# New ranks for a kernel's queues: a two-layer transformer on one core, with warm-up transposes and first scores ahead of first values

## The chip, the core and the metric

The kernel runs on one core of a Trainium2 chip. A core has five instruction queues that run side by side and wait for each other through semaphores: TensorE (PE in the profile: matrix products and transposes through the array, with its weight loads as PEld), VectorE (DVE), ScalarE (ACT), GpSimd (POOL) and SyncE (SP, which here issues nearly all transfers; POOL issues the indirect ones). Each queue works strictly in the order in which the program lists its instructions.

The metric is the device time of one execution in microseconds (us). The kernel before took 1245.04 us, the median of 3 runs (1244.42 to 1253.15).

## What is computed

Two transformer layers over 4096 tokens (16 sequences of 256) of width 128, all in 32-bit floats. Both layers have attention and a mixture of 8 experts of which each token uses 2; a normalisation follows each of the four parts.

```python
x = L0_attn_x                                   # (16, 256, 128)
x = _layernorm(x + _L0_attn_ref(x, ...))        # 16 heads of 64, softmax over 256 keys
x = _layernorm(x + _L0_ffn_ref(x, ...))         # 8 experts 128 -> 256 -> 128, top 2, and a shared one
x = _layernorm(x + _L1_attn_ref(x, ...))        # over the 16 heads of 8 of one token
x = _layernorm(x + _L1_ffn_ref(x, ...))         # 8 experts 128 -> 512 -> 128, top 2
return x
```

Layer 0's attention begins with an RMS norm, scales q by 1/8 and is the usual one. Layer 1's is odd: the softmax of a token runs over its own 16 heads, so scores and sums are small products within one token and are done element by element on VectorE and GpSimd, not as matrix products on TensorE. The expert layers take, for each token, the two largest of eight router probabilities, and add the two experts' outputs with those weights.

## The kernel before

**Tiles.** The tokens lie in 8 groups of 512 (`xg[0]` to `xg[7]`), each as 128 partitions by 4 chunks. Layer 0's attention runs over units: 128 pairs (a pair of heads in one sequence), 16 to a group. A unit has scores on PE (`scores`, L557, into `s`), the row maximum on DVE (`nm`, L533), the exponential on ACT (`pr`, L539), a reciprocal on DVE (`rs`, L550), the scaling of `pr` by it on POOL (L554), eight transposes on PE (`turn`, L587), copies of these out of PSUM (`pT`), the product with the values (`attended`, `po`, L608) and its copy (`oT`). A unit's transposes and products are issued three units after its scores (`LAG = 3`). Copies out of PSUM go through `copied` (L258), which gives each one to DVE (L266) or ACT (L268), whichever the planner believes is free first.

**Experts.** Most tokens go through the expert layers in waves (`WAVES`): layer 0 has waves 0 to 3, layer 1 has waves 0 to 2. A wave is routed (`route`, some 30 small DVE steps that end in each token's row numbers `r_pi`, L848); `send` (L891) scatters each token's row twice into a list in DRAM by indirect DMAs from POOL (L900); `lists` (L964) works through that list in tiles of 128 rows, with each tile's expert weights fetched by SP at a register's address (`wa`, `wb`), transposes (`px`), first products (`ph`, L1093), the GELU on ACT, second products (`po_e`, L1113) and a store into `outs`; `gathered` (L915) brings each token's two results back by indirect DMAs from POOL (`y`, L929). Only one wave's list runs at a time. `shared` (L1148) is layer 0's shared expert. The last 256 tokens use all 8 experts densely instead (`sequence`, `dense`).

**Layer 1's attention.** `chunk1` (L1196) handles 128 tokens: products of q and k on DVE (`qk_prod`), their sums (`sc`), the maximum, its subtraction on POOL or DVE (L1240), the exponential, products with v on POOL or DVE (`av_prod`, L1287), their sums and the scaling. Where the heads are over (`"over" in end`) and PE is `SUMS` us behind DVE in the planner's clock, both kinds of sums may be matrix products with the identity instead.

**What sets the order.** The whole program is written out at build time by a planner. Every piece of work (a unit's softmax, a wave's routing, a copy) is a Python generator, a *strand*; at each `yield` it says when its next step could start and on which engine. `everything` (L318) takes again and again the strand with the smallest start, and issues its next step:

```python
best = min(starts, key=lambda c: (max(c[0] - c[1].key[0], first), c[1].key[1:]))[1]
```

Here `key[0]` is a head start in us and `key[1]` a rank that breaks ties, both from the table `KEYS` (L147) by the kind of work: `"softmax": (rank, time)`. `PACE` gives the rank of the heads' main strand for each half group, `COPY`, `FAVOUR`, `SWITCH` and `SWITCH_BACK` bias the choice between engines and the wish to change ACT's function table. The planner's clock advances by charges written in the code (`work("DVE", 2.3, at)`): they are not measured at run time, they only decide the order. What it issues to a queue stays in that order on the chip, whatever the real times are.

**The start.** SP loads `x0`, `wq`, `wk`, `wv` and the rest in a fixed order. `normalised` (L463) makes the first normalised tokens; PE transposes them (`t_h`, L489) and a copy makes `hT`; from it come q and k (`projected`, L502, `pq`, `pk`) and v (`values`, L520, `pv`). `prepared` (L437) scales `wq` on DVE and writes the routing's constants on POOL; both are already issued behind the first norm here. `attention0` (L662) is the heads' main strand.

Of the kernel before, what the change touches and what calls it, by code (L numbers as in the profile page):

```python
# [9 lines left out]
FP = mybir.dt.float32  # L10
# [5 lines left out]
P = 128  # L16
D = 128
NTOK = 16 * 256
GT = 512
# [18 lines left out]
def two_layers(  # L38
# [71 lines left out]
    ident = const.tile([P, P], FP, tag="ident", name="ident")  # L110
    make_identity(nc, ident)
    mhalf = const.tile([P, NC], FP, tag="mhalf", name="mhalf")
    nc.gpsimd.memset(mhalf, -0.5)
# [20 lines left out]
    def cleared(layer, w):  # L134
# [12 lines left out]
    KEYS = {  # L147
        "copy qk": (-0.47, 0.098),
        "copy v": (-1.837, 0.311),
        "copy p": (-0.447, 0.289),  # L150
        "copy o": (-1.827, 0.05),
        "softmax": (-0.929, 0.15),
        "softmax 2": (-1.083, 0.3),
        "summed": (-2, 0.423),
        "normalised": (0.064, 0.401),
        "heads": (-0.036, 0.211),
        "w route": (0.209, 0.074),
        "w send": (-1.218, 0.245),
        "w shared": (-0.01, 0.358),
        "w loads": (-0.331, 0.017),  # L160
        "w turns 0": (-1.333, 0.096),
        "w turns 1": (0.218, 0.164),
        "w firsts 0": (-1.281, 0.243),
        "w firsts 1": (-0.641, 0.323),
        "w gelu": (-0.628, -0.115),
        "w seconds 0": (-0.513, 0.357),
        "w seconds 1": (0.844, 0.265),
        "w stored": (0.739, 0.057),
        "w gathered 0": (0.711, 0.093),
        "w gathered 1": (-0.147, -0.105),  # L170
        "w qkv": (0.126, -0.312),
        "w attention1": (0.364, 0.299),
        "w attention1 2": (1.784, 0.157),
        "w sums": (0.147, 0.241),
        "w normed": (-1.691, 0.205),
        "d loads": (-0.333, 0.978),
        "d route": (0.685, 0.221),
        "d firsts": (-0.122, -0.8),
        "d gelu": (-1.017, 0.988),
        "d seconds": (-0.245, -0.179),  # L180
        "d added": (-0.775, 1.421),
        "d normed": (0.891, 0.233),
    }
    PACE = [-0.064, 2, 0.528, -1.037, -1.955, -0.986, 0.284, 1.781]
    PACE += [1.065, 0.72, 1.611, 1.611, 1.069, 1.069, 1.469, 1.415]
    now = [0]
    COPY = -0.0
    SUMS = 14.742
    FAVOUR = -0.033
    SWITCH, SWITCH_BACK = 0.42, 0.949  # L190
    window, unit = [0, 0.0, 1.0], [P]
# [188 lines left out]
    def normed(y, o, tag, at):  # L380
# [21 lines left out]
        nc.gpsimd.tensor_scalar(nb, nb, -1.0, 1.0, ALU.mult, ALU.mult)  # L402
        at = work("POOL", 0.5, at)
        for c in range(n):
# [32 lines left out]
    def prepared():  # L437

        yield 4.0, "DVE"
        nc.vector.tensor_scalar(wq_s, wq_s, DH**-0.5, None, ALU.mult)  # L440
        end["wq"] = work("DVE", 0.75)
        yield after(("h", 0)), "POOL"
        nc.gpsimd.iota(falling, pattern=[[-1, NE]], base=NE, channel_multiplier=0, allow_small_or_imprecise_dtypes=True)
        nc.gpsimd.memset(earlier, 1.0)
        nc.gpsimd.affine_select(
            earlier, earlier, pattern=[[1, P]], compare_op=ALU.is_gt, fill=0.0, base=0, channel_multiplier=-1
        )
        nc.gpsimd.memset(ones, 1.0)


        nc.gpsimd.tensor_tensor(earlier, earlier, ones, ALU.subtract)
        nc.gpsimd.memset(going, 1.0)
        nc.gpsimd.memset(going[:, :, 0:1], 0.0)
        nc.gpsimd.memset(both, 0.0)
        nc.gpsimd.memset(upto, 0.0)
        for e in range(NE):
            nc.gpsimd.memset(upto[:, e, 0 : e + 1], 1.0)
        nc.gpsimd.iota(count, pattern=[[1, NTM]], base=0, channel_multiplier=0, allow_small_or_imprecise_dtypes=True)
        nc.gpsimd.iota(count128, pattern=[[P, CM]], base=0, channel_multiplier=0, allow_small_or_imprecise_dtypes=True)
        nc.gpsimd.memset(clear, 0.0)  # L460
        end["prepared"] = work("POOL", 9.0)

# [199 lines left out]
    def attention0():  # L662
        yield from projected(0, 0, wq_s, "q", qT)
        yield from projected(0, 0, wk_s, "k", kT)
        for c in range(NC):
            yield from values(0, 0, c)
        clears = [(0, 0), (0, 1), (1, 0), (0, 2), (1, 1), (0, 3), (1, 2)]
        for u in range(len(UNITS) + LAG):
# [4 lines left out]
            if g < NG:  # L673
# [27 lines left out]
                if i == 1 and 0 < g < LAST:  # L701
                    yield from values(g, 0, 3)
                yield from scores(u)
            if u >= LAG:
                yield from attended(u - LAG)
# [41 lines left out]
    def chosen(r, lg, layer, C, at):  # L747
# [33 lines left out]
        for k in range(2):  # L781
# [7 lines left out]
            nc.vector.tensor_tensor(first[:, k], eq, best.unsqueeze(2).to_broadcast(full), ALU.is_equal)  # L789
            at = work("DVE", 1.0 + 0.03 * C, at)  # L790
            yield at, "DVE"
        return first, pb, at

    def route(r, lg, layer, C, NT, at):
# [53 lines left out]
        nc.vector.tensor_copy(r.pos, pos)  # L848
        r.at = at = work("DVE", 2.3, at)
        begin(send(r), key("w send", w))  # L850
# [13 lines left out]
        if layer == 0:  # L864
# [15 lines left out]
            nc.vector.tensor_tensor(r.w[:, :, 0:NE], m.rearrange("p e c -> p c e"), pb, ALU.mult)  # L880
            r.weighed = work("DVE", 1.8, at)

# [313 lines left out]
    def chunk1(w, c, o, qv, kv, at, sums):  # L1196
# [57 lines left out]
        def reciprocals(at):  # L1254
            yield at, "DVE"
            nc.vector.tensor_reduce(rs, sc1, AX.X, ALU.add)
            nc.vector.reciprocal(rs, rs)
            mine["rs"] = work("DVE", 0.6, at)

# [399 lines left out]
```

## Time and profile before

One execution was profiled. It took 1250.27 us; its span, from the first to the last instruction, is 1248.6 us, and the mean granted clock of PE is 0.943 of full speed.

| | PE | DVE | ACT | POOL |
|---|---|---|---|---|
| busy, us | 1104.1 | 878.0 | 736.9 | 680.5 |
| share of the span | 88% | 70% | 59% | 54% |
| share of the chain that ended last | 49% | 21% | 6% | 14% |

Some times of this execution: the first scores start at 16.4 us; the maximum of unit 48 is taken at about 251 us, just after wave 0 of layer 0 has been routed; that of the last unit, 127, at about 864; the last product of the heads' output ends at 881; layer 1's three waves are routed by 924, 1038 and about 1132 us.

The page's rows are read as follows. A digit in a row of 40 slices is the busy share of that slice in tenths (a slice is 31 us); the DMA row is the mean share of 16 transfer engines. A row of a group gives the source line, the engine, the operation, the tile written and the tiles read, shapes and count, then the total busy time, the mean of one in ns, and the idle time of the engine just before these instructions with what ended it. A busy PE is not PE at its peak, since products are pipelined. Idle time of an engine counts only where something waits for that engine.

### The profile page before, as it was taken

The numbers are of one execution on the slowest core, as the hardware profiler recorded it, in microseconds if no ns is written. First come the engines' busy times: TensorE is split into PE (matmuls) and PEld (weight loads), VectorE is DVE, ScalarE is ACT, GpSimd is POOL, SyncE is SP. The second block draws the span as 40 slices with busy tenths as digits, with TensorE's granted clock in tenths as the row PEclk, the third lists the DMA queues.
The fourth block names the chain that finished last, engine by engine and source line by source line (L and its number), as shares of the span: only waits on it lengthen the run. The fifth ranks groups of instructions, "written<-read, shape, count | busy, mean of one in ns | idle before, by whom it ended". The sixth has DMA issues, their size and how long they took to land.

```text
span 1248.6 us, 22246 instructions
## 1 busy us (share of the span) xinstructions
PE 1104.1 (88%) x7175; PEld 795.3 (64%) x7175; DVE 878.0 (70%) x1748; ACT 736.9 (59%) x2086; POOL 680.5 (54%) x1059
## 2 busy tenths in 40 slices
PE   7999999979999999888999778998577998887985
PEld 3566665647665566656665456765455887887885
DVE  3766677634268897298789988779888779784433
ACT  5656566546757866477666567665346556544443
POOL 4434344372186647333765653485758827557654
PEclk9999999989999999789999889998768999888998
DMA  9800000033310003133000304213526879677981
GB/s 267 246 1 1 2 2 1 1 119 102 102 35 6 1 1 96 40 94 98 28 8 1 100 28 137 73 31 103 174 83 190 271 217 287 198 212 215 263 250 57
DMA packets 181527, 129.23 MB, mean 104 GB/s; under 512 B 12442, under 2 KB 165795, under 8 KB 181411
## 3 DMA queue, kind: packets, MB, share of 16 engines
q1 hardware_dynamic: 173730, 112.06, 30.4%
q0 software_dynamic: 7680, 15.74, 4.0%
q8 instruction: 58, 0.95, 0.3%
q14 instruction: 59, 0.48, 0.1%
HBM read 95.64 MB, written 32.11 MB: 102 GB/s over the span
## 4 chain that ended last, share of the span: by engine, by line
PE 49%; DVE 21%; POOL 14%; ACT 6%; issue 5%; DMA 4%; SPq 0%; ACTq 0%; POOLq 0%; DVEq 0%
PE s L570 8%; PE po L608 7%; POOL rows L900 7%; PE t L587 7%; PE ph L1093 3%; PE pv L524 3%; PE po_e L1113 3%; DVE qk_prod L1211 3%; PE pq L506 3%; PE pk L506 3%; PE py L625 3%; DMA y<-outs,r_pi 3%; DVE o L1262 3%; DVE sc L1215 2%; ACT pr L539 2%
## 5 line engine op out<-in xcount | busy, mean ns | idle before, releaser
L554 POOL TENSOR_SCALAR pr<-pr,rs 128x256 f32<-128x256 f32 x512 | 254.9, 515 | 329.4 <-DVE rs L550 237.7
L539 ACT ACTIVATE pr<-s,nm 128x256 f32<-128x256 f32 x512 | 235.6, 476 | 18.3 <-DVE nm L533 15.7
L533 DVE TENSOR_REDUCE nm<-s 128x4 f32<-128x1024 f32 x128 | 155.6, 1218 | 71.4 <-PE s L570 70.6
L1093 PE MATMUL ph<-xqT,wa 128*128 128x128 f32 x1000 | 139.1, 296 | 22.7 <-ACT h L1072 7.0
L587 PE MATMUL t<-ident,pr 128*128 128x128 f32 x1024 | 144.3, 282 | 6.7 <-POOL pr L554 4.6
L929 POOL DMA_INDIRECT y<-outs,r_pi x120 | 122.2, 1018 | 51.3 <-issue 23.4
L900 POOL DMA_INDIRECT rows<-x,r_pi x120 | 131.9, 1099 | 33.2 <-issue 20.8
L1093 PEld LDWEIGHTS ph<-xqT,wa 128*128 128x128 f32 x1000 | 129.6, 206 | 30.8 <-ACT h L1072 11.5
L608 PE MATMUL po<-pT,v 128*64 128x256 f32 x1024 | 142.4, 394 | 7.7 <-DVE kT L266 2.4
L587 PEld LDWEIGHTS t<-ident,pr 128*128 128x128 f32 x1024 | 112.9, 143 | 52.3 <-POOL pr L554 29.6
L570 PEld LDWEIGHTS s<-kT,qT 64*128 64x128 f32 x896 | 77.1, 186 | 85.2 <-issue 72.9
L570 PE MATMUL s<-kT,qT 64*128 64x256 f32 x896 | 127.0, 402 | 0.8 <-ACT pr L539 0.8
L266 DVE COPY pT<-t 128x512 f32<-128x512 f32 x146 | 95.4, 684 | 43.0 <-PE t L587 42.7
L268 ACT COPY oT<-po 128x256 f32<-128x256 f32 x103 | 38.3, 372 | 128.2 <-PE po L608 128.2
L608 PEld LDWEIGHTS po<-pT,v 128*64 128x64 f32 x1024 | 64.0, 136 | 67.4 <-issue 18.7
L539 ACT ACTIVATION_READ_ACCUMULATOR pr<-s,nm 128x1 f32 x512 | 106.2, 207 | 0.0
L1287 POOL TENSOR_TENSOR av_prod<-sc,qkv 128x1024 f32<-128x1024 f32 x28 | 70.8, 2535 | 60.6 <-ACT sc L1249 49.7
L1211 DVE TENSOR_TENSOR qk_prod<-qkv 128x1024 f32<-128x1024 f32 x64 | 82.3, 1286 | 10.1 <-ACT qkv L268 9.9
L268 ACT COPY pT<-t 128x512 f32<-128x512 f32 x110 | 61.2, 589 | 38.3 <-PE t L587 38.1
L1262 DVE TENSOR_REDUCE o<-av_prod 128x64 f32<-128x1024 f32 x64 | 76.1, 1205 | 6.0 <-POOL av_prod L1287 5.7
L1215 DVE TENSOR_REDUCE sc<-qk_prod 128x128 f32<-128x1024 f32 x64 | 78.1, 1220 | 2.2
L1113 PE MATMUL po_e<-wb,h 128*128 128x128 f32 x648 | 77.9, 279 | 1.7 <-ACT h L1066 1.4
(229 smaller groups left out, 1966.9 us busy)
## 6 DMA issues: line engine op xcount, KB each, us to landing
wa<-in_w_dram SPq DMA_DIRECT2D x176, 128.0 KB
wa<-in_w_dram SPq DMA_DIRECT2D x81, 256.0 KB
wb<-in_w_dram SPq DMA_DIRECT2D x81, 256.0 KB
xq<-rows SPq DMA_DIRECT2D x37, 256.0 KB
outs<-yq SPq DMA_DIRECT2D x37, 256.0 KB
rows<-clear SPq DMA_DIRECT2D x4, 1472.0 KB
rows<-clear SPq DMA_DIRECT2D x1, 2496.0 KB
rows<-clear SPq DMA_DIRECT2D x2, 1216.0 KB
```

Source lines behind the costliest of these rows:

```text
L533: nc.vector.tensor_reduce(nm[u], s, AX.X, ALU.max, negate=True)
L539: nc.scalar.activation(pr[u][:, i, :], s[:, i, :], AF.Exp, bias=nm[u][:, i : i + 1], accum_out=su[u][:, i : i + 1],)
L554: nc.gpsimd.tensor_scalar(pr[u][:, i, :], pr[u][:, i, :], rs[:, i : i + 1], 1.0, ALU.mult, ALU.mult)
L570: nc.tensor.matmul(sc[u][:, j, qc, :], q[part, ts(qc, P)], k[part, :], start=True, stop=True,)
L587: nc.tensor.transpose(t[:, kc, ts(qc, P)], pr[u][:, 2 * j + qc, ts(kc, P)], ident)
L608: nc.tensor.matmul(po[j * DH : (j + 1) * DH, :], vs[g, p // 4, 2 * b + kc][:, ts(h, DH)], pT[u][j][:, kc, :], start=(kc == 0), stop=(kc == 1),
L900: i = nc.gpsimd.indirect_dma_start(out=rows[layer][w][:, :], out_offset=bass.IndirectOffsetOnAxis(ap=r.pos[:, k, c : c + 1], axis=0), in_= ...
L929: nc.gpsimd.indirect_dma_start(out=y, out_offset=None, in_=outs[layer][w][:, :], in_offset=bass.IndirectOffsetOnAxis(ap=r.pos[:, k, c0 + c ...
L1093: nc.tensor.matmul(ph[:, q - q0, c, :], was[i, q][0][:, c, :], xTs[i][0][:, q, :], start=True, stop=True)
L1113: nc.tensor.matmul(po[:, q, :], hs[i, q][0][:, c, :], wbs[i, q][0][:, c, :], start=(c == 0), stop=(c == nh - 1))
L1211: nc.vector.tensor_tensor(m, q3[:, ts(j, HALF)].unsqueeze(2).to_broadcast(full), k3.unsqueeze(1).to_broadcast(full), ALU.mult)
L1262: nc.vector.tensor_reduce(o[:, c, ts(j, P // 2)], m.rearrange("p h d g -> p (h d) g"), AX.X, ALU.add)
```

## The change

The change adds 28 transposes of the identity on PE ahead of everything else (nothing reads them), moves the four value projections of the first group's first half from ahead of the first scores to behind the scores of units 0 and 1 (two each), and replaces the planner's numbers: all entries of `KEYS`, `PACE`, `COPY`, `SUMS`, `FAVOUR`, the two switch values, and seven charges.

```diff
     ident = const.tile([P, P], FP, tag="ident", name="ident")
     make_identity(nc, ident)
+
+    t = ps_t.tile([P, GT], FP, tag="t", name="t_busy")
+    for c in range(28):
+        nc.tensor.transpose(t[:, ts(c % NC, P)], ident, ident)
     mhalf = const.tile([P, NC], FP, tag="mhalf", name="mhalf")
...
-        "copy v": (-1.837, 0.311),
-        "copy p": (-0.447, 0.289),
+        "copy v": (0.797, 0.337),
+        "copy p": (-0.251, 0.567),
...
-        "softmax": (-0.929, 0.15),
-        "softmax 2": (-1.083, 0.3),
+        "softmax": (0.46, 0.411),
+        "softmax 2": (-1.944, 0.253),
...
-        "w route": (0.209, 0.074),
-        "w send": (-1.218, 0.245),
+        "w route": (1.025, 0.203),
+        "w send": (0.283, 0.121),
...
-        "w attention1": (0.364, 0.299),
+        "w attention1": (1.523, 0.038),
...
-    PACE = [-0.064, 2, 0.528, -1.037, -1.955, -0.986, 0.284, 1.781]
-    PACE += [1.065, 0.72, 1.611, 1.611, 1.069, 1.069, 1.469, 1.415]
+    PACE = [-0.535, 1.803, -0.789, 1.43, -1.644, -1.523, 0.233, 1.863]
+    PACE += [2, 2, 1.526, 1.378, 0.905, 1.647, 1.284, 2]
     now = [0]
-    COPY = -0.0
-    SUMS = 14.742
-    FAVOUR = -0.033
-    SWITCH, SWITCH_BACK = 0.42, 0.949
+    COPY = -0.091
+    SUMS = 15.528
+    FAVOUR = 0.255
+    SWITCH, SWITCH_BACK = 0.844, 1.787
...
-        at = work("POOL", 0.5, at)
+        at = work("POOL", 0.4, at)
...
-        end["prepared"] = work("POOL", 9.0)
+        end["prepared"] = work("POOL", 4.0)
...
         yield from projected(0, 0, wk_s, "k", kT)
-        for c in range(NC):
-            yield from values(0, 0, c)
...
                 yield from scores(u)
+                if u < 2:
+                    for c in (2 * u, 2 * u + 1):
+                        yield from values(0, 0, c)
...
-            at = work("DVE", 1.0 + 0.03 * C, at)
+            at = work("DVE", 1.3 + 0.05 * C, at)
...
-        r.at = at = work("DVE", 2.3, at)
+        r.at = at = work("DVE", 2.6, at)
...
-            r.weighed = work("DVE", 1.8, at)
+            r.weighed = work("DVE", 2.1, at)
...
-            mine["rs"] = work("DVE", 0.6, at)
+            mine["rs"] = work("DVE", 0.7, at)
```

The computation is the same. Since every choice of the planner can fall otherwise, the order of all queues differs. What the two built programs show, counted by engine:

| work | before: DVE / ACT / POOL | after: DVE / ACT / POOL |
|---|---|---|
| copies `pT` | 146 / 110 / - | 109 / 147 / - |
| copies `v` | 15 / 49 / - | 47 / 17 / - |
| `av_prod` | 36 / - / 28 | 22 / - / 42 |
| subtraction of the maximum | 24 / - / 8 | 7 / - / 25 |
| rows normalised (`xn`, and `x` after the three norms) | 38 / 90 / - | 14 / 114 / - |
| loads of a function table | - / 56 / - | - / 52 / - |

PE has the same products in both, beside the 28 transposes; SP has 1088 instructions in both. On PE, the list of wave 0 of layer 0 stands between units 48 and 59 before, and between 60 and 75 after; that of wave 1 between 84 and 91, and between 76 and 83; that of wave 2 between 108 and 119, and from 116 on. On POOL, the 16 sends of each of the waves 0, 1 and 2 stand in these runs, with scalings of `pr` between the runs: before 16; 8, 4, 4; 16. After: 2, 3, 3, 8; 15, 1; 6, 2, 1, 2, 5.

## The prediction

> **What bounds the kernel now.** I read the page first: busy shares, then the 40 slices of each engine and of DMA in tenths, then the chain of waits.
>
> ```profile
> PE 1104.1 (88%) x7175; PEld 795.3 (64%) x7175; DVE 878.0 (70%) x1748; ACT 736.9 (59%) x2086; POOL 680.5 (54%) x1059
> ...
> DVE  3766677634268897298789988779888779784433
> ...
> DMA  9800000033310003133000304213526879677981
> ```
>
> No engine bounds the whole span. TensorE (PE) has half of the chain that ended last (49%), but the later half of DVE's row is at 8 and 9 tenths, and the DMA row fills up only in the last quarter. So I asked for the busy time in stretches cut at events of the program (columns: stretch, length, then each engine's busy time and instructions, PE clock, DMA share): the first list of experts is routed near 250 us, the heads end near 865, most rows of layer 1's first wave are sent near 955.
>
> ```profile
> core 0: us, PE busy (x) PEld busy (x) DVE busy (x) ACT busy (x) POOL busy (x), PEclk, DMA share, GB/s
> ...
> 48.00:250.00 202.00, 200.71 (x1293) 123.02 (x1294) 138.28 (x247) 117.76 (x425) 81.78 (x172) 1.00 0.05 15
> 250.00:865.00 615.00, 558.12 (x3555) 378.10 (x3550) 453.88 (x840) 404.60 (x1202) 338.42 (x524) 0.96 0.20 59
> 865.00:955.00 90.00, 65.87 (x345) 49.74 (x345) 80.85 (x169) 47.39 (x111) 61.53 (x85) 0.77 0.44 131
> 955.00:1200.00 245.00, 206.41 (x1554) 192.52 (x1555) 164.42 (x383) 121.90 (x214) 155.55 (x190) 0.92 0.82 244
> ```
>
> To 250 us PE is never idle: only less PE work helps. From 250 to 865 PE idles 57 us and loses more at a lower clock. From 865 to 955 DVE is at 80.85 of 90 us: it is the bound. From 955 on DMA is at 0.82 with the expert weights, 244 GB/s where the best 50-us slices have 270: a floor that no rank moves.
>
> **Part 1, the start.** The timeline of PE:
>
> ```profile
> 6.72 1.11 PE L489 MATMUL t_h<-ident,xn 128*128 128x128 f32 x4 [6.72 <-DVE xn L477]
> 8.61 2.08 PE L506 MATMUL pq<-hT,wq 128*128 128x512 f32 x2 [0.78 <-ACT hT L498]
> 10.48 1.50 PE L506 MATMUL pk<-hT,wk 128*128 128x512 f32 x2
> ...
> 15.42 1.02 PE L506 MATMUL pq<-hT,wq 128*128 128x512 f32 x2
> ```
>
> The same projection takes 2.08 us at 8.6 and 1.02 at 15.4, so PE starts at half speed and is up to speed within 5 us of its first work. The 28 transposes need only the identity, ready at about 1.4 us. At the half-speed pitch of t_h (0.22 us between starts) they take 6.2 us if none is sped up and end near 7.6, 0.9 us after t_h could start. The Trainium skill (TensorE: Matmul & The Clock Gate, Part 1) says that about 3.4 us of activity release a half-rate gate: by it the last dozen would be fast and the block would end at about 6.5. Trace alone: -1.0 (pq) -0.5 (pk) +0.9 = -0.6 us; with the rule: -1.0 -0.5 -0.4 (t_h) = -1.9. I take the rule; the profile's granted clock says 1.00 here and can't decide it.
> The first four value projections (3.77 us) move behind the scores of units 0 and 1, so those scores (16.4 us now) start some 4 us earlier. The PE work stays; what can be won is PE's idle time between 16.4 and 48 us, 31.60 - 30.59 = 1.0. Against it, the first hT goes from ACT to DVE, behind the scaling of wq (0.69): +0.5 at most. Part 1 is -1.9 - 1.0 + 0.5 at most: I take -2.5, with bounds 0 and -4. Nothing is issued on SP by it. The words "constants and wq's scaling behind the first norm" and "head sums may use TensorE" change nothing: both programs have the first already, and neither issues one matmul for such sums, the condition never holding. These two are worth 0.
>
> **Part 2, what the new ranks move between engines**, counts of the two built programs times rows of the trace:
>
> ```profile
> L1287 POOL TENSOR_TENSOR av_prod<-sc,qkv 128x1024 f32<-128x1024 f32 x28 | 70.8, 2535 | 60.6 <-ACT sc L1249 49.7 <-DVE o L1262 8.3 <-ACT pr L539 2.5
> ...
> L1287 DVE TENSOR_TENSOR av_prod<-sc,qkv 128x1024 f32<-128x1024 f32 x36 | 54.5, 1516 | 0.0
> ```
>
> DVE: 37 pT copies less at 0.684 (-25.3), 32 v copies more at 0.687 (+22.0), 14 av_prod less (-21.2), 17 subtractions less at 0.432 (-7.3), 24 normalised rows less at 0.28 to 0.35 (-8.0), small ones +2: -38 us. POOL: +14 x 2.535 +17 x 0.632 +5 pairs of bias terms (2.3) = +48. ACT: +37 x 0.589 -32 x 0.587 +24 rows (11.2) -4 table loads of 1.283 = +9. The copies cancel. What counts is that av_prod, subtractions and rows leave DVE: 36.5 us, 13 of the 14 av_prod before the heads end. Only where DVE is the bound does this shorten anything: of the 10-us windows from 685 to 825 and 845 to 955 about half show DVE at 9.0 or more. Half of 36 is -17; bounds 0 (if PE's order holds the pace anyway) and -36. POOL at 54% takes its 48 us as long as no pr waits behind an av_prod (2.5 us each).
> A rule speaks against the move. The DVE av_prod costs 1516 ns where the same shape in qk_prod costs 1286, so something slows it by 0.23. The Trainium skill (GPSIMD Engine Reference, 1. Specifications) says that POOL's SBUF interfaces are shared with VectorE and contend with its instructions of two SBUF inputs. By the row alone, the move costs DVE nothing more; by the rule, 35.5 us more of POOL av_prod meet such DVE work, which is 137 us (qk_prod and av_prod) of 878, for 16%: up to +5.6. I take +2.
>
> **Part 3, where the lists stand.** A wave's rows are sent by POOL, and pr of the heads queues behind. In before, wave 0's 16 sends stand in one block (251.6 to 271.9 us), and so do wave 2's 16 (696.6 to 718):
>
> ```profile
> 260.00:270.00 10.00, 6.34 (x30) 3.93 (x28) 1.34 (x4) 4.48 (x11) 8.46 (x17) 1.00 0.60 188
> 270.00:280.00 10.00, 7.55 (x23) 4.04 (x24) 1.42 (x3) 3.70 (x12) 7.14 (x15) 0.66 0.22 69
> ...
> 705.00:715.00 10.00, 6.91 (x25) 4.97 (x24) 9.65 (x28) 3.75 (x5) 8.47 (x17) 0.64 0.61 186
> 715.00:725.00 10.00, 3.65 (x15) 2.32 (x16) 8.95 (x9) 2.88 (x7) 9.62 (x14) 0.51 0.24 72
> ```
>
> PE idle plus busy time times (1 - clock): 8.7 us in the first pair, 13.7 in the second. In after wave 0's sends stand as 2, 3, 3, 8 and wave 2's as 6, 2, 1, 2, 5 with pr between. But wave 1's, 8, 4, 4 before, become 15 and 1: 7 more in a row at 1.27 us is 9 us of hold, of which I charge 5. Of the 22.4 I take half, as these experts' DMAs and products are late next: -11 +5 = -6, bounds -20 and +5. Wave 0's list also moves from units 48 to 58 to units 60 to 73, beside wave 1's; the same tiles, rows and weight loads go through SP wave by wave as before, so I give that no size of its own.
>
> **Part 4, the tail.** Layer 1's routing of its first wave ends (r_pi) at 924.2 us, the second's at 1037.9, and the last send of the second at 1062.6; its rows are fetched by SP at 1086: about 22 us of slack after landing. In after DVE has more between these two routings: 22 qk_prod and score sums where there were 13 (9 x 2.51 = 22.6), 20 o sums for 10 (12.1), 2 av_prod (3.0), four or five each of four small steps (6.2): about +43 us. DVE was idle for 25 of the 121 us from 912 to 1033 (busy 95.83). So the second routing comes 18 to 43 later, less the slack: 0 to +21 on the end. I take +8. Queued behind it on POOL are 16 sends, behind those SP's fetches, and PE's products for 23 tiles.
>
> **The sum.** -2.5 -17 +2 -6 +8 = -15.5 us. The profiled execution took 1250.3 us (span 1248.6, 1.7 around it), 5 above the median of 1245.0; the differences carry over, so 1250.3 goes to 1234.8 and the median, 1245.0, to **1229**.
>
> **The rivals.**
> A. As summed, 1229, own range 1217 to 1240. For it: DVE's row near 9 tenths before and after 865. Also, the planner's charges for routing get nearer the trace (the position step takes 3.0 us from 248.65 to 251.66, charged 2.3 before and 2.6 now; constants take 2.7, charged 9.0 and now 4.0), so a queue's order should fit real arrival better. 0.42.
> B. The stalls between 250 and 865 really go: all of the 22 us and 25 of DVE's 36, tail +8: about -33, 1212. Against it: what a stall hides is usually another. 0.13.
> C. PE's work keeps its pace and DVE's relief is hidden; only the start is won: 1242. For it: 200.71 of 202 us. Against: that holds only to 250. 0.15.
> D. Slower: the second routing of layer 1 becomes the wait. It decides once it comes over 22 us later after the first than now. With no lead won before, and 12 gathers of wave 2 (12.2 us) now standing on POOL after the last pr, where three av_prod (7.6) leave: -2.5 +21 +5 = +23.5, 1268; a pr held behind wave 1's 15 sends or an av_prod adds to it. For it: the 43 us counted above, on an engine already at 80%. 0.30.
>
> **The numbers.** Runs of before spread from 1244.4 to 1253.2, so about 1% is what can be told from no change. Faster by over 1% (below 1232.6): 0.27 of A and B, 0.40. Within: 0.15 of A, C, 0.02 of D, 0.32. Slower: 0.28. The range from 1205 to 1265 leaves out the far half of B and the upper part of D.
>
> **What would show it.** Start: pq near 1.0 us at about 8.6, first scores near 11.5. Part 2: DVE near 840 busy, POOL near 725, and the first routing of layer 1 (r_pi) at 925 - 18 or so. Part 3: no 20-us POOL block of sends at wave 0. Part 4: from that r_pi to the next more than 121 us, and to the first fetch of its rows no more than 170 (161 now). I am wrong if the first r_pi of layer 1 isn't earlier, or if DMA falls below 0.6 between the two waves' lists.

## The result and the profile after

The changed kernel took 1266.43 us, the median of 4 runs (1258.0 to 1270.07), beside 1249.1 us for the kernel before on the same chip (the 1245.0 of the prediction is from 3 runs, this from 4): ratio 1.013, 95% interval 1.0089 to 1.0172. Two more sets of runs gave 1.0113 and 1.0107. The prediction, 1229, had the wrong sign. Its rival D stood at 1268; as a difference it foresaw +23.5 us, and +17.3 was measured, so the two times lie as near as they do in part because the base rose by 4 us.

The profiled execution took 1267.45 us (span 1265.7, clock 0.944). From its page come the busy shares, DVE's and DMA's slices, and the shares of the chain that ended last.

```profile
PE 1121.9 (89%) x7203; PEld 807.4 (64%) x7203; DVE 864.1 (68%) x1694; ACT 740.0 (58%) x2105; POOL 718.4 (57%) x1100
...
DVE  5666566765237358878968988666688998876333
...
DMA  8800000003030444210000210334667676776981
...
PE 60%; DVE 15%; POOL 11%; ACT 7%; issue 4%; DMA 3%; SPq 0%; ACTq 0%; DVEq 0%; POOLq 0%
```

DVE has 14 us less than before and POOL 38 us more, yet the span is 17 us longer. The same stretches that were shown of the kernel before tell where (columns: stretch, length, busy time and instructions of PE, PEld, DVE, ACT and POOL, clock, DMA share, GB/s):

```profile
48.00:250.00 202.00, 200.49 (x1286) 122.96 (x1284) 131.13 (x224) 127.06 (x448) 81.84 (x172) 1.00 0.06 16
250.00:865.00 615.00, 554.20 (x3441) 374.26 (x3441) 421.68 (x759) 389.96 (x1180) 346.31 (x533) 0.94 0.18 53
865.00:955.00 90.00, 71.42 (x434) 54.49 (x433) 64.30 (x176) 47.75 (x119) 68.05 (x100) 0.91 0.65 194
955.00:1200.00 245.00, 197.46 (x1386) 178.79 (x1386) 193.07 (x384) 120.38 (x208) 160.58 (x183) 0.90 0.73 213
```

Between 250 and 865, DVE is busy 32 us less, and PE is no busier (554.20, 558.12 before). From 955 to 1200, DVE is busy 29 us more (193.07, 164.42 before), PE 9 us less, and DMA's share falls from 0.82 to 0.73.

The events divide the loss. Layer 1's first routing (its `r_pi`) comes at 921.7 us, 2.5 earlier than before. From there to the end it is 344.0 us, 324.4 before: +19.6, and -2.5 + 19.6 is the 17.1 us by which the span grew. Of these 19.6, the interval to the second routing has +35.6 (149.3, 113.7 before), that to the third -7.1, the rest -8.9.

The kernel before took 1249 us in some sets of runs and 1303 to 1316 in others (the second group, below), so each ratio is to the runs of before in the same set, and times of single profiles are compared within a group only.

### The profile page after: what moved, and what is told of

The parts are those of the page before. It is cut to its first block, busy times and chain, and to the rows that moved or that the text cites. A ratio compares the mean times of both kernels' runs of the same rounds, so it can differ in the third digit from the quotient of the medians.

```text
span 1265.7 us, 22301 instructions
## 1 busy us (share of the span) xinstructions
PE 1121.9 (89%) x7203; PEld 807.4 (64%) x7203; DVE 864.1 (68%) x1694; ACT 740.0 (58%) x2105; POOL 718.4 (57%) x1100
## 3 DMA queue, kind: packets, MB, share of 16 engines
q1 hardware_dynamic: 173730, 112.06, 30.1%
## 4 chain that ended last, share of the span: by engine, by line
PE 60%; DVE 15%; POOL 11%; ACT 7%; issue 4%; DMA 3%; SPq 0%; ACTq 0%; DVEq 0%; POOLq 0%
PE po L612 9%; PE s L574 9%; PE t L591 9%; POOL rows L905 5%; PE ph L1098 4%; PE py L629 4%; PE pv L528 4%; PE pk L510 4%; PE po_e L1118 3%; PE pq L510 3%; POOL av_prod L1292 2%; DMA y<-outs,r_pi 2%; DVE o L1267 2%; DVE qk_prod L1216 2%; POOL y L934 2%
## 5 line engine op out<-in xcount | busy, mean ns | idle before, releaser
L1098 PE MATMUL ph<-xqT,wa 128*128 128x128 f32 x1000 | 141.9, 299 | 31.9 <-ACT xqT L272 10.9
L612 PE MATMUL po<-pT,v 128*64 128x256 f32 x1024 | 146.7, 405 | 15.4 <-DVE oT L270 4.7
L905 POOL DMA_INDIRECT rows<-x,r_pi x120 | 125.1, 1043 | 50.7 <-issue 21.1
L591 PEld LDWEIGHTS t<-ident,pr 128*128 128x128 f32 x1024 | 115.9, 146 | 48.4 <-issue 27.0
L272 ACT COPY pT<-t 128x512 f32<-128x512 f32 x147 | 83.9, 587 | 56.6 <-PE t L591 55.5
L1292 POOL TENSOR_TENSOR av_prod<-sc,qkv 128x1024 f32<-128x1024 f32 x42 | 101.9, 2436 | 21.9 <-ACT sc L1254 11.8
L270 DVE COPY pT<-t 128x512 f32<-128x512 f32 x109 | 74.0, 688 | 53.1 <-PE t L591 52.9
L1118 PE MATMUL po_e<-wb,h 128*128 128x128 f32 x648 | 80.9, 286 | 2.3 <-ACT h L1071 1.5
L1118 PEld LDWEIGHTS po_e<-wb,h 128*128 128x128 f32 x648 | 78.8, 202 | 4.5 <-ACT h L1071 2.2
```

What stands on the lines that cost most here:

```text
L272: nc.scalar.copy(o, i)
L591: nc.tensor.transpose(t[:, kc, ts(qc, P)], pr[u][:, 2 * j + qc, ts(kc, P)], ident)
L612: nc.tensor.matmul(po[j * DH : (j + 1) * DH, :], vs[g, p // 4, 2 * b + kc][:, ts(h, DH)], pT[u][j][:, kc, :], start=(kc == 0), stop=(kc == 1),
L905: i = nc.gpsimd.indirect_dma_start(out=rows[layer][w][:, :], out_offset=bass.IndirectOffsetOnAxis(ap=r.pos[:, k, c : c + 1], axis=0), in_= ...
L1098: nc.tensor.matmul(ph[:, q - q0, c, :], was[i, q][0][:, c, :], xTs[i][0][:, q, :], start=True, stop=True)
L1118: nc.tensor.matmul(po[:, q, :], hs[i, q][0][:, c, :], wbs[i, q][0][:, c, :], start=(c == 0), stop=(c == nh - 1))
```

## The experiments

**First question: did DVE's load in the heads set the first routing of layer 1?** One kernel shortens DVE's work there and leaves every queue in its order:

```diff
-                nc.vector.tensor_reduce(sc1[:, ts(j, HALF)], m, AX.X, ALU.add)
+                if routed1[0].listed == INF:
+                    nc.vector.tensor_copy(sc1[:, ts(j, HALF)], m[:, :, :, 0])
+                else:
+                    nc.vector.tensor_reduce(sc1[:, ts(j, HALF)], m, AX.X, ALU.add)
```

> The kernel before with the 40 score sums of layer 1's attention beside layer 0's heads, up to the first routing of layer 1, made one-term copies of 0.50 us in place of 1.22 us (left out: 7 of 8 terms of these scores): 28.8 us of DVE's time leave the heads and every queue keeps its order. The prediction's second step counted half of what leaves DVE there as time: by it the first routing of layer 1 comes 12 to 15 us sooner (910 to 912) and the end as much. Rival 'TensorE's own work sets the heads': within 3 us of 924, and the end within 4 us.

Measured: 1246.96 us, ratio 0.9988 (0.9965 to 1.001). The first routing came at 919.1. Its stretches:

```profile
250.00:865.00 615.00, 561.77 (x3576) 379.03 (x3572) 429.74 (x857) 408.77 (x1217) 341.85 (x529) 0.96 0.21 61
865.00:919.00 54.00, 34.81 (x145) 23.14 (x146) 44.94 (x101) 19.93 (x36) 33.45 (x45) 0.71 0.45 132
```

DVE is busy 429.74 us there where it was 453.88, and next to nothing came of it: the 12 to 15 us of the theory lie far outside the interval, which ends at 4.4 us. The first routing, 919.1, is 5 us earlier than in the profile of before, 2 more than the rival allowed, but another profile with before's order up to there has it at 921.4, and six profiles of the changed kernel's order spread over 11 us there, so this can't be told from nothing. The heads' pace does not hang on this load of DVE, although its row stands at 8 and 9 tenths.

**The start alone.** The 28 transposes, put into the kernel before:

```diff
     make_identity(nc, ident)
+    t = ps_t.tile([P, GT], FP, tag="t", name="t_busy")
+    for c in range(28):
+        nc.tensor.transpose(t[:, ts(c % NC, P)], ident, ident)
```

> The kernel before with the 28 transposes alone added; every queue keeps its order. Theory (the start's terms): the first projection pair falls from 2.08 us to near 1.0, the first scores start 1 to 2 us earlier, and PE, never idle to 250 us, carries that to the heads: 0 to 2 us faster, the same within noise. Rival (the block is too long): t_h waits for it and the start is up to 0.9 us later; also the same within noise. Neither can make the 17 us.

Measured: 0.997 (0.9947 to 0.9994). This is a gain of 4 us of 1316. In its trace the maximum of unit 0 is taken at 16.0 us, 17.6 before.

**The ranks as a whole.** `KEYS`, `PACE` and the five other numbers were exchanged, in both directions; then two entries alone, in the changed kernel:

```diff
-        rank, time = KEYS[what]
+        rank, time = (KEYS2 if w == 2 and what in ("w turns 0", "w firsts 0") else KEYS)[what]
```

> The changed kernel with the ranks and biases of before (KEYS, PACE, COPY, SUMS, FAVOUR, the switch values); warm-ups, value order and charges stay changed. If the new ranks cost the 1.3%, this is back near before (1240 to 1255). If the charges or the value order cost it, it stays near 1266. DVE has 20 qk_prod between the first two routings of layer 1 in this order (13 in before, 22 in after): if that count decides the end, it is slow in spite of the old ranks, with an interval between these routings near 140 us and an end near 1260.

> The kernel before with the changed ranks and biases alone. If the ranks cost the 1.3%, it is near 1266 or above. This order has 13 qk_prod between the first two routings of layer 1, as before, but 23 between unit 122 and the end of the heads: if the DVE work between the two routings decides, that interval is near 114 us and the tail as short as before, and the loss, if any, lies ahead of the heads' end.

> The changed kernel where only wave 2 of layer 0 gets before's keys for its transposes and first products (two rows of the table). By the program's order its list moves from beside units 119 to 125 to beside units 114 to 118 (111 to 115 in before) and 14 qk_prod stand between the first two routings of layer 1 instead of 22; nothing changes up to unit 108. Theory (the late list of wave 2 pushes attention of its tokens into the tail, so the second routing is late): its last store comes some 30 us earlier, the interval between the routings falls from 149 to 110 to 125, and the end is 10 to 20 us ahead of the changed kernel, level with before. Rival (the loss is made elsewhere): the end stays within 5 us of the changed kernel.

Measured: 1.0664 (1.0605 to 1.0724), 1.1133 (1.1071 to 1.1195) and 1.0722 (1.0666 to 1.0779). All three are far slower than both kernels. A set of ranks belongs to one set of charges and one start: taken over by another program, it plans another order, and here a worse one each time. The intervals between layer 1's first two routings were 181, 159 and 138 us; expected were near 140, near 114 and 110 to 125. With the two entries exchanged, the heads' last `py` is at 968 us (894 in the changed kernel), although the edit was meant for one wave's list. So such exchanges can't attribute a cost; from here on the edits keep the queues' order, or change it only behind the first routing of layer 1.

**Second question: what holds the second routing?** Groups of the changed kernel between layer 1's first and second routing (last columns: busy us, mean ns, idle before):

```profile
L1220 DVE TENSOR_REDUCE sc<-qk_prod 128x128 f32<-128x1024 f32 x22 | 26.8, 1220 | 0.8
L1216 DVE TENSOR_TENSOR qk_prod<-qkv 128x1024 f32<-128x1024 f32 x22 | 26.8, 1219 | 0.0
L1267 DVE TENSOR_REDUCE o<-av_prod 128x64 f32<-128x1024 f32 x20 | 23.7, 1203 | 2.0 <-POOL av_prod L1292 1.9
...
L1292 POOL TENSOR_TENSOR av_prod<-sc,qkv 128x1024 f32<-128x1024 f32 x12 | 30.1, 2520 | 8.4 <-ACT sc L1254 5.7 <-DVE o L1267 2.7
```

and of the kernel before:

```profile
L1215 DVE TENSOR_REDUCE sc<-qk_prod 128x128 f32<-128x1024 f32 x13 | 15.9, 1220 | 0.4
...
L1262 DVE TENSOR_REDUCE o<-av_prod 128x64 f32<-128x1024 f32 x10 | 12.0, 1213 | 2.3 <-POOL av_prod L1287 2.2
...
L1287 POOL TENSOR_TENSOR av_prod<-sc,qkv 128x1024 f32<-128x1024 f32 x5 | 12.2, 2441 | 20.6 <-ACT sc L1249 20.6
```

So 22 score products stand there in place of 13, 20 head sums in place of 10, and 12 of POOL's `av_prod` in place of 5. The first theory was that DVE's longer work is the price. Two edits that keep all orders: between these two routings, score sums and head sums issued twice in the kernel before; in the changed kernel, score sums made copies of one term, in two sets of runs (the edit shown above, with the condition `routed1[0].listed < INF and routed1[1].listed == INF`).

> The kernel before, same order, where DVE does the sums of layer 1's attention twice between the first two routings of layer 1 (12 score sums and about 10 output sums more, some 27 us). Theory: DVE had 25 us idle there and the second list 22 us of slack, so the second routing is 5 to 27 us later and the end 3 to 15 us later. Rival (DVE is not the wait in the tail): the end moves by less than 3 us.

> The changed kernel, all queues in the same order, where the 22 sums of score products that DVE does between the first two routings of layer 1 are replaced by a copy of the first of the eight terms (so layer 1's attention and what follows is another function of those tokens): about 22 us less DVE work just there. Theory (the second routing is the wait): the interval of 149 us between the two routings falls to 125 to 132, the second list starts some 15 us earlier, the end comes 8 to 20 us earlier, near 1250. Rival (the first list's own pace is the bound, through SP's order of loads or DMA): the second routing comes earlier, but the last store of the first list stays near 1109 us and the end within 4 us of 1266.

> The thinned sums once more (22 sums of score products between the first two routings of layer 1 are one-term copies, so layer 1's attention of those tokens is another function), now beside the changed kernel on the same chip. Theory (the second routing is the wait): end 8 to 20 us ahead of the changed kernel. Rival (first list's own pace, or DMA): within 4 us of it.

> The changed kernel itself, unaltered, so that the edits of it can be read against it on one chip: before took 1316 us on the chip of the first experiments, not 1249, so only kernels of one chip are compared. Ratio to before between 1.009 and 1.03. Its 149 us between the first two routings of layer 1 and the 124 us from the first fetch to the last store of wave 2's list in layer 0 should show again, scaled by what before is longer.

Doubled: 1.0196 (1.0142 to 1.0251), the interval between the routings 132.8 us in place of 113.7. The second sums stand as a group of their own:

```profile
L1215 DVE TENSOR_REDUCE sc<-qk_prod 128x128 f32<-128x1024 f32 x13 | 15.9, 1219 | 0.4
...
L1217 DVE TENSOR_REDUCE sc<-qk_prod 128x128 f32<-128x1024 f32 x12 | 14.6, 1220 | 0.4
```

So 27 us more of DVE work bought 19 us of interval and some 23 us of time. In the kernel before, more work on DVE there delays the routing by some 0.7 us for each us, and cost more than was expected (3 to 15 us). Thin sums in the changed kernel did not bring what this suggests: 1.0326 (1.0268 to 1.0385) in a set of the second group without the changed kernel, and 1.0125 (1.0071 to 1.018) beside 1.0113 (1.0081 to 1.0144) for the changed kernel itself, where 8 to 20 us less were expected. Their group shows that the time did leave DVE:

```profile
L1221 DVE COPY sc<-qk_prod 128x128 f32<-128x128 f32 x22 | 11.0, 501 | 0.8
```

It is 11.0 us in place of 26.8, and the interval stayed at 149.0. DVE's time alone does not hold the second routing of the changed kernel. The traces suggest why: the chain of waits, followed back from the second routing to the first by the rule of the page, spends 49 to 56 us on DVE, 40 to 60 on POOL, 10 to 19 on ACT and 3 to 27 on PE in the three profiles of the changed kernel. With thin sums it has 33 on DVE, 43 on POOL and 38 on PE: the chain went over to other engines, and its length stayed.

**The place in TensorE's queue.** Counted in the traces, 829 matmul records lie between the two routings, 704 before. That made a second theory: more matrix products of the first list were put ahead of it. One edit of the choice in `everything` moves it, behind the first routing only; `chained` holds the keys of wave 2's attention, norms and routing:

```diff
-            best = min(starts, key=lambda c: (max(c[0] - c[1].key[0], first), c[1].key[1:]))[1]
+            ahead = 1.8 if routed1[0].listed < INF and routed1[1].listed == INF else 0.0
+            best = min(
+                starts,
+                key=lambda c: (max(c[0] - c[1].key[0] - (ahead if c[1].key in chained else 0.0), first), c[1].key[1:]),
+            )[1]
```

> The changed kernel; only between the first two routings of layer 1 the strands that lead to the second one (layer 1's attention of wave 2, its norms and scores) are ranked 1.8 us ahead. TensorE's queue then has 372 matmul instructions of its program between the first and the second routing in place of 445 (375 in the kernel before), 340 between the second and third in place of 267, and 357 after the third as before the edit; vector work and everything up to the first routing stay. Theory 'place in TensorE's queue': the second routing comes late because 70 more matmuls were put ahead of it, so it comes 15 to 25 us after the first routing sooner (interval 124 to 134 us, 149 now), the second list's rows are there when the first list ends, the stall of 7.3 us before px at the change of lists goes, and the end comes 8 to 17 us sooner: 1247 to 1258, ratio to before 0.998 to 1.007. Rival 'pace': the first list is slow because of POOL's and the loads' pace, whatever the order; the routing comes sooner but the end stays within 4 us of the changed kernel: 1261 to 1270, ratio 1.009 to 1.017. Rival 'attention chain': the second routing waits for its own chain through POOL, DVE and ACT; then the interval stays above 143 us and the end within 4 us.

> The kernel before; the same strands ranked 0.05 us ahead in the same stretch, which happens to put 478 matmul instructions between the first two routings of layer 1 in place of 375, 191 between the second and third in place of 318, and 409 after the third in place of 385; all before the first routing stays. Theory 'place in TensorE's queue': the interval grows from 114 to some 145 us and a gap opens when the first list is done, as in the changed kernel: 10 to 20 us slower, 1259 to 1270, ratio 1.008 to 1.016. Rivals 'pace' and 'attention chain': within 4 us of the kernel before.

> The kernel before; the same strands ranked 0.25 us ahead in the same stretch: 307 matmul instructions between the first two routings of layer 1 in place of 375, 388 to the third in place of 318, 383 after it in place of 385. Theory 'place in TensorE's queue': the second list was in time before (no stall over 2 us at the change of lists), so an earlier second routing buys nothing more: within 5 us of the kernel before, 1244 to 1254. Should even the kernel before have waited there, it gains 5 to 12 us. Rivals: within 4 us.

> The changed kernel with the same strands 1.7 us ahead: 316 matmul instructions between the first two routings of layer 1 in place of 445, 320 to the third in place of 267, and so 449 after the third in place of 357: both late routings come earlier in TensorE's queue. Theory 'place in TensorE's queue': at least as good as with the second alone: 1244 to 1258, ratio 0.996 to 1.007; and if the third routing was late as well, below 1250. Rivals 'pace' and 'attention chain': within 4 us of the changed kernel, 1261 to 1270.

They gave 1.0224 (1.0168 to 1.028), 1.0513 (1.0462 to 1.0563), 1.0183 (1.0136 to 1.0231) and 1.0585 (1.0529 to 1.0641), in the second group and without the changed kernel in the set. So it was run beside the first of them again:

> The changed kernel as it is, as the comparison on this chip: ratio to before 1.010 to 1.015 where before is near 1249; where before is near 1316, as it was on another chip, 1.025 to 1.04 by the changed kernel with thin sums there.

> The changed kernel with the second routing of layer 1 at 372 matmul instructions of TensorE's queue behind the first in place of 445, beside the changed kernel on the same chip. Theory 'place in TensorE's queue': 8 to 17 us faster than the changed kernel, no stall over 3 us before px at the change from the first list to the second (7.3 us in the changed kernel). Rival 'pace': within 4 us of the changed kernel.

> The same with thin sums: the 22 score sums of layer 1's attention between the first two routings are one-term copies of 0.50 us in place of sums of 1.22 us (left out there: 7 of 8 terms of these scores), which takes 15.8 us off DVE in the stretch and leaves the order alone. If DVE is what holds the second routing once TensorE's queue does not, the end comes 4 to 12 us before that of the kernel without thin sums; if not, within 4 us.

Measured: 1.0107 (1.0052 to 1.0162), 1.0255 (1.021 to 1.0299) and 1.0216 (1.0171 to 1.0262). The theory falls. Thin sums took 9 us off the median in this order (1272.8 us against 1281.9; the runs overlap, 1266 to 1279 and 1275 to 1284), as was expected if DVE holds the routing once TensorE's queue does not. The table is counted in the traces, between layer 1's first and second routing; the last column is the time from the first to the end.

| kernel | `qk_prod` | matmul records | interval, us | to the end, us |
|---|---|---|---|---|
| before | 13 | 704 | 113.7 | 324.4 |
| before_thin_heads | 13 | 704 | 116.0 | 324.9 |
| before_doubled_sums | 13 | 704 | 132.8 | 345.1 |
| changed kernel, three profiles | 22 | 825 to 833 | 148.8 to 151.5 | 341.9 to 344.6 |
| after_thin_sums_2 | 22, thin | 819 | 149.0 | 344.5 |
| after_second_up_2 | 20 | 688 | 154.6 | 360.6 |
| after_second_up_thin | 20, thin | 688 | 148.7 | 353.9 |
| *second group:* warmups_alone | 13 | 704 | 124.6 | 358.3 |
| before_second_up | 13 | 572 | 110.3 | 385.8 |
| before_second_late | 22 | 897 | 189.0 | 427.4 |
| after_second_up | 20 | 688 | 154.7 | 393.5 |
| after_thin_sums | 22, thin | 824 | 170.8 | 410.0 |
| after_two_up | 22 | 583 | 162.3 | 440.6 |

With some 145 records fewer ahead of it, the second routing came no sooner, so their count is not what sets it. The rival 'attention chain' foresaw that (interval above 143 us), though not the end, 19 us later than the changed kernel in place of 4 at most. Across the rows the interval goes with the number of `qk_prod` that stand in it, 110 to 133 us with 13 and 148 to 189 with 20 or 22; the count of matmuls doesn't order it (583 gave 162 us, 704 gave 125, both in the second group). The count is not all: the kernel before with the changed ranks has 13 as well, and 159 us. And an early second routing is no gain in itself: before_second_up has the shortest interval and 1.8% more time; its third comes 126.4 us later in place of 94.1.

In after_second_up_2 the chain ran into a collision, seen in the timelines of DVE (first two rows) and POOL (last row; columns: start, us, operation):

```profile
939.95 1.22 DVE L1274 TENSOR_REDUCE o<-av_prod 128x64 f32<-128x1024 f32 x1 [2.22 <-POOL av_prod L1299]
941.08 4.50 DVE L1299 TENSOR_TENSOR av_prod<-sc,qkv 128x1024 f32<-128x1024 f32 x1
...
937.57 6.92 POOL L1299 TENSOR_TENSOR av_prod<-sc,qkv 128x1024 f32<-128x1024 f32 x3
```

POOL's three `av_prod` end at 944.49; DVE's, started at 941.08, ends at 945.58, 1.1 us later. A DVE product takes 1.2 us when POOL has none, so it waited until POOL was through. The 32 sends of the first list, which stand on POOL among the `av_prod`, took 60 us in that kernel from the first to the last (921.8 to 982.0), 52 in the changed one beside it (914.8 to 966.4).

**POOL's share.** Its 12 `av_prod` there cover half the keys; their sums run twice over that half in the first kernel, and in the second once, with thin score sums besides:

```diff
-            (nc.gpsimd if e == "POOL" else nc.vector).tensor_tensor(
-                m,
-                sc1[:, ts(j, HALF)].unsqueeze(2).to_broadcast(full),
-                v3.unsqueeze(1).to_broadcast(full),
+            few = NH1
+            if e == "POOL" and routed1[0].listed < INF and routed1[1].listed == INF:
+                few = NH1 // 2
+            part = [P, HALF, DH1, few]
+            (nc.gpsimd if e == "POOL" else nc.vector).tensor_tensor(
+                m[:, :, :, 0:few],
+                sc1[:, ts(j, HALF), 0:few].unsqueeze(2).to_broadcast(part),
+                v3[:, :, 0:few].unsqueeze(1).to_broadcast(part),
```

> The changed kernel; the 12 av_prods that POOL works between the first two routings of layer 1 cover 8 of the 16 keys (left out: the other 8 keys of these head sums), and the sums over them run twice over the 8, so that DVE keeps its time. POOL loses some 12 x 1.2 = 14 us there, every queue keeps its order. Theory 'left-over attention on DVE and POOL together' (22 qk_prods and 20 av_prods stand between the two routings, 13 and 12 in the kernel before): POOL alone buys a part, second routing 3 to 10 us sooner and the end 3 to 8 us sooner than the changed kernel's 1264. Rival 'pace of the first list on TensorE and its loads': within 4 us of 1264 where before is near 1249.

> The same 12 av_prods over 8 of 16 keys with their sums once over the 8, and the 22 score sums as one-term copies (left out: 8 of 16 keys in these head sums, 7 of 8 terms in these scores): some 14 us leave POOL and 16 + 12 x 0.6 = 23 us leave DVE between the first two routings, queues in the same order. Theory 'left-over attention on DVE and POOL together': the second routing comes 12 to 25 us sooner after the first (124 to 137 us, 149 to 151 in the changed kernel) and the end 8 to 17 us sooner: 1247 to 1256. Rival 'pace of the first list': interval above 143 us, end within 4 us of 1264.

Measured: 1.0209 (1.0168 to 1.025) and 1.0271 (1.0232 to 1.031), in the second group. POOL's group fell from 30.1 to 17.2 us, by 13:

```profile
L1297 POOL TENSOR_TENSOR av_prod<-sc,qkv 128x512 f32<-128x512 f32 x12 | 17.2, 1439 | 12.3 <-ACT sc L1254 7.8 <-DVE o L1268 3.5 <-ACT r_scratch L772 1.0
```

The intervals were 155.8 and 157.2 us, 170.8 with thin sums alone in another set of that group, where before was 13 us slower. This could point at POOL, but the changed kernel was not run in either set, and relieving DVE as well added nothing, against the theory. It stays a hint.

## Why the prediction was wrong

The sum was to give -15.5 us, and the profile has +17.1. Parts 1 to 3 were to give -23.5 up to the first routing of layer 1 and gave -2.5; Part 4 was to cost 8 and cost 19.6. The step that failed is Part 2; Part 3 failed with it, and Part 4 was mis-sized.

**Part 1, the start (-2.5): right, too small.** The timeline of PE after:

```profile
1.43 4.58 PE L115 MATMUL t_busy<-ident 128*128 128x128 f32 x28 [1.43 <-POOL ident masks.py:199]
6.79 0.92 PE L493 MATMUL t_h<-ident,xn 128*128 128x128 f32 x4 [0.78 <-DVE xn L481]
8.64 1.13 PE L510 MATMUL pq<-hT,wq 128*128 128x512 f32 x2 [0.93 <-DVE hT L499]
...
11.49 1.14 PE L574 MATMUL s<-kT,qT 64*128 64x256 f32 x8
```

`pq` takes 1.13 us in place of 2.08, the first scores start at 11.49 as foreseen (11.5), and unit 48's maximum is taken at 246.6 us, 4.7 earlier. The block took 4.58 us, not the 6.2 of the trace's own pitch: its starts are 0.213 us apart at first and 0.109 from the 14th on, about 2.8 us after the first (4.0 us in the trace with the transposes alone). So the transposes did speed up within it, as the rule of the Trainium skill (TensorE: Matmul & The Clock Gate, Part 1) had it, with its 3.4 us between the two values; `t_h` was not delayed. "Constants and wq's scaling" and "head sums" were worth 0, as said: both programs issue the same there.

**Part 2, DVE's relief (-17): this step failed.** It took DVE's busy windows for the bound. Two stretches, from the maximum of unit 48 to that of the last unit and from there to the first routing, in the kernel before (first two rows) and the changed one (columns as above):

```profile
251.30:864.30 613.00, 556.26 (x3542) 377.09 (x3541) 452.01 (x837) 403.41 (x1198) 337.97 (x522) 0.96 0.20 59
864.30:924.20 59.90, 38.62 (x161) 25.73 (x162) 53.24 (x115) 23.88 (x53) 34.87 (x46) 0.70 0.46 139
...
246.60:875.70 629.10, 567.93 (x3535) 383.92 (x3537) 429.42 (x777) 397.76 (x1201) 351.38 (x541) 0.95 0.18 54
875.70:921.70 46.00, 36.64 (x192) 24.93 (x192) 31.92 (x111) 23.01 (x54) 36.27 (x55) 0.93 0.70 210
```

In the heads DVE has 23 us less, and they take 16 us more. PE is busy 12 us longer there on nearly the same count of products; what slows it was not settled. That DVE's load does not set the pace of the heads is shown by before_thin_heads without the new order: the bound "0 (if PE's order holds the pace anyway)" was right for them. "Half of the windows are at 9 tenths" was read as "DVE is the bound in half of them"; a high share alone does not show that anything waits.

Behind the heads the stretch is 14 us shorter, in all the profiles with the changed order (45 to 46 us, 59 to 60 before). There the kernel before has 5 `qk_prod`, 6 `av_prod` and their sums between the steps of the routing; the changed kernel has none. They stand behind the first routing now, where 22 `qk_prod` were 13. This fits DVE as the bound of that stretch, but no edit moved only that work. So the 2.5 us are the sum of 4.7 won at the start, 16 lost in the heads, and 14 won where attention had been put off, to stand in the way of the second routing.

POOL has 718 us (725 expected), DVE 864 where 840 were expected. Part of this lies in the term of +2 for POOL and DVE in each other's way. The big products show none of it: those of DVE that overlapped POOL's `av_prod` or subtractions were 20 before (mean 1.91 us, the others 1.23) and 20 after (1.91, the others 1.25). But smaller two-input work of DVE grew at the same count: `x<-y,r_gate,x` (120) from 49.3 to 54.5 us, `o<-o,c_rs` (32) from 9.3 to 14.8. Over all two-input operations of DVE, the time above what the same line and shape usually takes is about 31 us before and 42 after, an estimate from the two traces. How much of it lay on the path is open.

**Part 3, the sends' runs (-6): nothing won.** The holds moved rather than went. Just behind the sends of waves 0 and 2, the changed kernel has these:

```profile
730.00:740.00 10.00, 7.71 (x18) 3.25 (x18) 9.86 (x11) 6.39 (x12) 9.27 (x15) 0.66 0.06 20
...
315.00:325.00 10.00, 5.49 (x15) 1.90 (x14) 2.13 (x4) 6.31 (x13) 3.70 (x7) 0.66 0.24 74
```

Idle and slow clock make 4.9 and 6.4 us there. Reckoned in the same way over 250 to 865 us, from the rows shown, the loss is some 94 us after and 79 before.

**Part 4, the tail (+8): right mechanism, mis-sized.** The interval grew by 35.6 us, inside the 18 to 43 foreseen. Its two rows, before and after:

```profile
924.20:1037.90 113.70, 96.95 (x706) 87.36 (x704) 89.95 (x191) 67.00 (x136) 73.74 (x95) 0.92 0.72 216
...
921.70:1071.00 149.30, 121.52 (x829) 107.81 (x830) 131.68 (x241) 81.64 (x159) 99.58 (x112) 0.89 0.67 201
```

DVE has 42 us more in it, as counted (43). POOL has 26 more, 18 of them `av_prod`, which the sum put at nothing. The sign "more than 121 us" was taken from another stretch, 912 to 1033; the interval itself was 113.7. The first fetch of the second list came 178.4 us after the first routing (161 before; at most 170 was foreseen): the slack took some 19 of the 36, and 17 reached that fetch. PE's timeline shows the wait itself:

```profile
1104.66 1.12 PE L1060 MATMUL px<-ident,xq 128*128 128x128 f32 x4 [7.27 <-DMA xq<-rows]
```

The first list is through and the second's rows aren't there; before, the longest wait of `px` was 2.1 us. This is rival D: the second routing becomes the wait once it comes over 22 us later. D got 0.30; the lead from Part 2 was to pay for it, and did not come. (Rival B's terms, with the rest of the sum, give -34.5, not -33; this changes nothing.) The reason given with D, DVE's 43 us more, is only half shown. In the kernel before, more DVE work delays the routing; in the changed kernel, less does not hasten it, since the chain of waits runs over DVE, POOL, ACT and PE by turns.

**Open.** Which work to take away so that the second routing of the changed kernel comes sooner was not found. That the interval goes with the attention work left over is shown by the counts, not by an edit that moves only that work ahead of the first routing; this wasn't tried. Nor is it known what makes the heads 16 us longer.

## What to carry to other kernels

Before a busy engine's relief is counted as time, shorten its work with every queue in the same order: here such a run shows next to nothing where the sum counted 17 us. In a kernel whose order a planner chooses, follow the work that is still undone at each hand-over: with attention put off behind the first routing, the stretch ahead of it was 14 us shorter and the one behind it 36 us longer. An order tuned for one set of charges isn't a setting that carries over: exchanged, it cost 7 to 11%.

## What the hardware showed unexpectedly

DVE products with two inputs in SBUF do not slow down beside POOL's products: the one that starts second waits. Of the 20 overlapping ones in the kernel before, 12 started while POOL was at work and ended 1.08 to 1.09 us after POOL's; 7 started first, took their usual 1.21 to 1.22 us, and POOL's product, 2.3 to 2.4 us long alone, ended 2.19 to 2.23 us after them; one started just as POOL ended. So the mean of 1.91 us above is a mix of two cases. The Trainium skill (Trainium Architecture — The Big Picture, What this means for kernel authors) calls the port pair that these two engines share an exclusive lock, and the trace agrees.
